# Two layers of attention and FFN on one core: in the second attention, two of four row tiles and of four probability tiles are transposed as 32x32 squares on VectorE and by DMA, and the last weights are loaded later, from GpSimd's queue

## The chip, the core and the metric

The kernel runs on one core of a Trainium2 chip. The metric is the device time of one execution in microseconds (us). The kernel before takes 454.63 us, the median of three runs (454.27 to 454.71).

## The reference

The input `x` is two sequences of 512 rows with 512 columns, float32. Two layers follow each other, and each is an attention and an FFN, each with a residual and a LayerNorm:

```
x = layernorm(x + L0_attn(x))     # memory read-out: elu(q)+1 against a given M and z, then Wo
x = layernorm(x + L0_ffn(x))      # ternary weights, silu(gate)*up, results truncated to int8
x = layernorm(x + L1_attn(x))     # one head of 128:
                                  #   q,k,v = x @ Wqkv + bqkv
                                  #   softmax(q k^T / sqrt(128)) v @ Wo + bo
x = layernorm(x + L1_ffn(x))      # (silu(x Wg^T) * (x Wu^T)) Wd^T, inner width 1376
```

The change is in the third line, `L1_attn`, and in when the weights of the fourth are loaded.

## The kernel before, in words

Everything is tiled by 128 partitions. A sequence `b` has four row tiles `xs[b][t]` (x_b_t below) of 128 rows by 512 columns; they stay in SBUF from the first layer to the last. The 1376 inner columns of the FFNs are 11 chunks, with weights `gu` (gate and up, 512 KB a chunk) and `wd` (down, 256 KB a chunk).

A matmul on TensorE contracts over the partitions, so a row tile has to be transposed before it can be multiplied with weights: its columns have to lie on the partitions. The kernel has two ways to do it.

- On TensorE: four 128x128 products with an identity into a PSUM bank, which VectorE or ScalarE copies to SBUF. `transposed` (L118) does so for four tiles of a sequence, 16 products.
- In squares: `nc.vector.transpose` turns each 32x32 square of a tile in its place, and `move_squares` (L301) moves the squares to where they belong, 16 DMAs of [32 partitions x tiles x 4 squares x 32 elements], one for each pair (i, j) of a source and a target group of 32 partitions. With `queues=3` the four DMAs with i == j are copies on VectorE instead, since these squares don't leave their partitions; four go on GpSimd's queue and eight on SyncE's. With `queues=2` the four go on GpSimd's queue too, which has eight then.

The stages around the change, in order:

1. The end of the first FFN (`f0_down`, `added`, `normed`, L888 to L990): for each row tile a down product on TensorE, truncation on ScalarE, sums and LayerNorm on VectorE, with the root on GpSimd. The first two tiles of sequence 0 are turned in squares (L963), the other two on TensorE (L981).
2. The second attention (L1128 to L1298), for b = 0 and then 1: queries and keys `pqk` (L1148), values `pv` (L1166), scores `psc` (L1099), their maxima on VectorE (`maxima`, L1102), exponentials on ScalarE (`exponentials`, L1111). Sequence 0's four probability tiles are turned in squares (L1180), sequence 1's rows and probabilities by `transposed` (L1131, L1287). `values` (L1206) multiplies the transposed probabilities with v into `pot`, `output` (L1228) the result with Wo, and `attended` (L1233) adds it to the row tile, divided by the sum of the exponentials. The bias `bo` is added to sequence 0's tiles by GpSimd (L1181) and to sequence 1's by four accumulating DMAs on GpSimd's queue (L1196), which stand behind a one-element copy `landed` (L1194) that reads what the last DMA of sequence 0's squares writes.
3. The second FFN (from L1299). Its products are done in three passes over operands that are split in an upper part (ScalarE) and rests (VectorE): `split_up` (L1056) for weights, `rows_room`, `turn_rows`, `rows_from_squares` for rows. The second sequence's rows are turned in squares again (`squares_r1`, L1308, `xt_f11`, L1315). `in_turn` is a chain that keeps VectorE's steps in a fixed order. A loop over `steps` (L1546) then goes through the chunks in the order of `turn` (L1046: 6 to 10, then 0 to 5), and splits weights two or more steps ahead of their use; the weights of chunk 2 are split after those of 6 to 10, 0 and 1, those of 3, 4 and 5 after that, and the down weights last.

The order of an engine's instructions is set when the program is built, by a scheduler; `with tc.issue_after(step)` puts what stands under it behind that step. GpSimd follows the program's own order. Each engine and each DMA queue runs its list in that order: an instruction that waits holds up what is behind it. DMAs of one queue use eight semaphores in turn.

The weights of the second FFN are loaded by SyncE: chunks 6 to 10 as soon as the first FFN has done with their room (L1009), then, behind the moves of sequence 0's first two tiles, all down weights and chunks 0 to 5 (L1011 to L1013). In SyncE's queue the moves of sequence 0's probabilities stand behind them.

Of the kernel before, what the change touches and what calls it, by code (L numbers as in the profile page):

```python
# [10 lines left out]
F32 = mybir.dt.float32  # L11
# [8 lines left out]
P = 128  # L20
B, S, HID = 2, 512, 512
NT = S // P
# [17 lines left out]
def kernel(  # L40
# [41 lines left out]
    def psum(name):  # L82
        return ps.tile([P, 512], F32, tag="mm", name=name)
# [152 lines left out]
    def branch(flag):  # L236
        return nc.values_load(flag[0:1, 0:1], engines=[PE], min_val=0, max_val=1)

    def up_weights(gu_in, name, chunks=range(len(CHUNKS))):
        gus = []  # L240
        for c in chunks:
            i, n = CHUNKS[c]
            gu = wffn.tile([P, 2, NK, n], F32, tag=f"gu{c}", name=f"gu{name}_{c}")
            at = 2 * HID * i
            nc.sync.dma_start(
                gu.rearrange("p a k i -> p (a k i)"),
                gu_in[at : at + 2 * HID * n].rearrange("(p f) -> p f", p=P),
            )
            gus.append(gu)
        return gus  # L250

    def down_weights(wd_in, name):
        wds = []
        for c, (i, n) in enumerate(CHUNKS):
            wd = wdp.tile([P, HID], F32, tag=f"wd{c}", name=f"wd{name}_{c}")
            nc.sync.dma_start(wd[:n], wd_in[i : i + n, :])
            if n < P:
                nc.gpsimd.memset(wd[n:], 0.0)
            wds.append(wd)
        return wds  # L260
# [497 lines left out]
    moved = move_squares(squares, xt1)  # L758
    wdp = ctx.enter_context(tc.tile_pool(name="wdp", bufs=1))
    with tc.issue_after(moved.ins):  # L760
        wds = down_weights(wd0_in, "0")
    with tc.tile_pool(name="f0", bufs=2) as f0:
        factors = {}

# [213 lines left out]
        for t in range(TURNED, NT):  # L978
            pt = psum(f"pt_a10_{t}")
            for k in range(NK):  # L980
                nc.tensor.transpose(pt[:, ts(k, P)], xs[0][t][:, ts(k, P)], ident)  # L981
            copies.append(
                nc.scalar.copy(xt_a10[1][:, t - TURNED], pt.rearrange("p (k i) -> p k i", k=NK))
            )
        added(i - 2)
        normed(i - 3)
        added(i - 1, behind=copies[-2:])
        normed(i - 2)
        for i in range(len(order), len(order) + 2):
            f0_down(i)  # L990

    def joined_weights(gu_in, c):

# [12 lines left out]
        nc.sync.dma_start(half.rearrange("p (k i) -> p k i", k=NK), up[:, :, : P // 2])  # L1006
        return full, half

    gus = up_weights(gu1_in, "1", range(6, len(CHUNKS) - 1))  # L1009
    gus.append(joined_weights(gu1_in, len(CHUNKS) - 1))  # L1010
    with tc.issue_after(moves_a.ins):  # L1011
        wds = down_weights(wd1_in, "1")
    gus = up_weights(gu1_in, "1", range(6)) + gus  # L1013

# [73 lines left out]

    probs = []

    def scores(b):

        qt, kt, _ = qkv[b]
        got = []
        for t in range(NT):
            p = psum(f"psc_{b}_{t}")
            nc.tensor.matmul(p, qt[:, ts(t, P)], kt, start=True, stop=True)  # L1099
            got.append((p, small.tile([P, 1], F32, tag="mx", name=f"mx_{b}_{t}", bufs=8)))  # L1100

        def maxima(tiles):  # L1102
            for t in tiles:
                p, mx = got[t]
                nc.vector.reduce_max(mx, p, AX.X)
                done = nc.vector.tensor_scalar_mul(mx, mx, -scale)
            return done

        return got, maxima

    def exponentials(b, got, behind={}):  # L1111
        sums = small.tile([P, NT], F32, tag="sums", name=f"sums_{b}")
        row = []
        for t, (p, mx) in enumerate(got):
            if t % 2 == 0:
                two = pair_tile(f"prob_{b}_{t}")
            e = two[:, t % 2, :]
            with ExitStack() as tied:
                if t in behind:
                    tied.enter_context(tc.issue_after(behind[t].ins))  # L1120
                moved = nc.scalar.activation(
                    e, p, AF.Exp, bias=mx, scale=scale, accum_out=sums[:, t : t + 1]
                )
            row.append(e)
        probs.append((row, sums))
        return moved

    qkv = []  # L1128
    for b in range(B):
        if b:  # L1130
            xt = transposed(xs[b], f"a1{b}")  # L1131
            with tc.issue_after(copies[-2].ins), tc.issue_after(copies[-1].ins):
                split_up(0, room0)
                split_up(1, room1[:6])
        qk = []
        qk2 = query_tile(f"qk_{b}")
        if b == 0:
            v2 = query_tile("v")
        pqk = [psum(f"pqk_{b}_{j}") for j in range(2)]
        for half in range(2 - b):  # L1140
            for j in range(2):
                for k in range(NK):
                    if b:
                        p, rows = pqk[j], xt[:, k, :]
                    else:
                        p = pqk[j].rearrange("p (h t i) -> p h t i", h=2, i=P)[:, half]
                        rows = xt_a10[half][:, :, k, :]
                    nc.tensor.matmul(  # L1148
                        p, wqkv[:, k, ts(j, D)], rows,
                        start=(k == 0), stop=(k == NK - 1),  # L1150
                    )
        for j, p in enumerate(pqk):
            s = qk2[:, j, :]
            moved = nc.scalar.activation(s, p, AF.Identity, bias=bqk[:, j : j + 1])
            qk.append(s)
        if b:
            pt0 = fp.tile([P, NT, NK, P], F32, tag="it10", name="pt_p0", bufs=1)
            move_squares(squares, pt0)
            pt0 = pt0.rearrange("p t k i -> p k t i")
        else:  # L1160
            table(AF.Exp, moved)
        v = v2[:, b, :].rearrange("p (t d) -> p t d", t=NT)
        for t in range(NT):
            p = psum(f"pv_{b}_{t}")
            for k in range(NK):
                nc.tensor.matmul(  # L1166
                    p[:, :D],
                    xt[:, k, ts(t, P)] if b else xt_a10[t // 2][:, t % 2, k, :],
                    wqkv[:, k, ts(2, D)],
                    start=(k == 0), stop=(k == NK - 1),  # L1170
                )
            nc.vector.tensor_add(v[:, t, :], bv, p[:, :D])
        qkv.append((qk[0], qk[1], v))
        if b == 0:
            got, maxima = scores(0)
            maxima(range(NT))
            exponentials(0, got)
            squares = fp.tile([P, NT, HID], F32, tag="it00", name="squares_p0", bufs=1)
            for t in range(NT):
                nc.vector.transpose(squares[:, t, :], probs[0][0][t])  # L1180
                nc.gpsimd.tensor_add(xs[0][t], xs[0][t], bo)  # L1181
# [5 lines left out]
            weight_upper(gus[turn[2]][:, a].rearrange("p k i -> p (k i)"), room2[3 * a])  # L1187

    got, maxima = scores(1)
    scaled_max = maxima(range(NT))  # L1190
    table(AF.Silu, exponentials(1, got))

    landed = small.tile([P, 1], F32, tag="off", name="landed")
    nc.gpsimd.tensor_copy(landed[2 * SQ : 3 * SQ], pt0[2 * SQ : 3 * SQ, NK - 1, NT - 1, P - 1 :])  # L1194
    for t in range(NT):
        nc.gpsimd.dma_start(xs[1][t], bo_in.to_broadcast([P, HID]), accum_op=ALU.add)  # L1196
    with tc.issue_after(scaled_max.ins):
        done = split_up(2, room2, True)
    with tc.issue_after(done.ins):
# [6 lines left out]
    def values(b, pt, cuts):  # L1206

        ot = ot2[:, b, :]
        w = S // cuts
        for i in range(cuts):  # L1210
            po = psum(f"pot_{b}_{i}")
            for k in range(NT):
                nc.tensor.matmul(  # L1213
# [70 lines left out]
        return pts, turned  # L1284

    values(0, pt0, 1)
    pt1 = transposed(probs[1][0], "p1").rearrange("p k (t i) -> p k t i", t=NT)  # L1287
    for t in range(NT):
        attended(0, t, output(0, t))
        norm_a1(0, t)  # L1290
    values(1, pt1, 2)
    for t in range(NT - 1):
        done = attended(1, t, output(1, t))
    rooms = [rows_room(0, "r0"), None]
    x3 = [row_blocks(rooms[0]), None]
    pts, turned = turn_rows(0)
    with tc.issue_after(turned.ins):
        p = output(1, NT - 1)  # L1298
    in_turn = Chain(done)  # L1299
    for pt, (h, m, _) in zip(pts, x3[0]):  # L1300
        in_turn(lambda: upper_lower(pt, h, m)[1])
    for t in range(NT - 1):
        in_turn(lambda: norm_a1(1, t))
    in_turn(lambda: attended(1, NT - 1, p))
    x = xs[1][NT - 1]
    stats = layernorm_stats(x, f"a11_{NT - 1}")
    in_turn.last = taken[f"a11_{NT - 1}"]
    squares = xtp.tile([P, NT, HID], F32, tag="xt", name="squares_r1")  # L1308
    for t in range(NT - 1):
        in_turn(lambda: nc.vector.transpose(squares[:, t, :], xs[1][t]))  # L1310
    in_turn(lambda: layernorm_apply(x, x, stats))
    in_turn(lambda: nc.vector.transpose(squares[:, NT - 1, :], x))
    for h, m, d in x3[0]:
        in_turn(lambda: crossed(d, h, m))
    xt_r1 = fp.tile([P, NT, NK, P], F32, tag="it10", name="xt_f11", bufs=1)  # L1315
# [230 lines left out]
    for i, (b, j) in enumerate(steps):  # L1546
# [6 lines left out]
            while len(held) > 1:  # L1553
                moved = finish_up()
        if i == 1:
            in_turn(lambda: split_up(AHEAD - 1, take(6)))
        elif i == 2:
            rooms[1] = rows_room(1, "r1")
            x3[1] = row_blocks(rooms[1])
            for k in range(NK):  # L1560
                with tc.issue_after(in_turn.last.ins):
                    uppers, in_turn.last = rows_from_squares(k)
        elif i == AHEAD:
            for h, m, d in x3[1]:
                in_turn(lambda: crossed(d, h, m))
# [80 lines left out]
```

## Time and profile before

| | |
|---|---|
| runs, median (lowest to highest) | 454.63 us (454.27 to 454.71) |
| the profiled execution's own time | 454.45 us |
| its span, first to last instruction | 452.7 us |
| TensorE clock granted (mean) | 0.999 |
| from 232.4 to 251.6 us: TensorE, VectorE, ScalarE, GpSimd busy | 19.20, 17.32, 10.11, 11.25 us |
| from 251.6 to 268.9 us: the same | 17.30, 14.83, 10.84, 3.95 us |
| DMA in the same two stretches | 136 and 40 GB/s |

A stretch's busy times tell which engine has room in it: TensorE has none in either, VectorE about two us in each, and GpSimd most of the second.

In the profile, PE is TensorE's matmuls and PEld its weight loads, DVE is VectorE, ACT ScalarE, POOL GpSimd, SP SyncE; a q behind the name is the engine's sequencer, which issues DMAs. L12 is line 12 of the kernel. Tile names are the program's, without the numbers behind an underscore: `pt_p` stands for the transposed probabilities of both sequences, PSUM and SBUF, `x<-in_bo` for the bias additions. A float32 product shows as two matmuls, so 16 transposes are x16 in the chain's rows, where each of them counts once, and 8 products of float32 by 512 columns are x16.

### The profile page before, as it was taken

The page shows a single profiled execution, that of the slowest core. Times are in us where ns is not written, and L with a number is a line of the kernel's source. Part 1 is how long each engine was busy: PE and PEld are TensorE (multiplying, and loading weights), DVE is VectorE, ACT ScalarE, POOL GpSimd, SP SyncE. Part 2 cuts the span into 40 slices and gives each one's busy share as a digit, 9 for nine tenths or more (in the row PEclk, how much of TensorE's full clock was granted, in tenths as well). Part 3 has the DMA queues.
Part 4 walks back from the last instruction along what each step waited for, and adds up shares of the span by engine and source line. Part 5 has one row for each costly group of instructions (what it writes and reads, how often), then busy time and mean ns, then how long its engine had stood idle before and what let it go on. Part 6 is the DMA issues. An engine that isn't in the chain of part 4 may idle for free.

```text
span 452.7 us, 5850 instructions
## 1 busy us (share of the span) xinstructions
PE 445.8 (98%) x1913; PEld 337.0 (74%) x1913; DVE 317.5 (70%) x634; ACT 259.7 (57%) x493; POOL 117.6 (26%) x164
## 2 busy tenths in 40 slices
PE   8999999999999999999999999999999999999995
PEld 8887753344587888888875578888888888888884
DVE  4976767877886898849898889545535447777524
ACT  5788995567467975567755645454645456442311
POOL 0300206566640059203384137000000000012111
PEclk9999999999999999999999999999999999999999
DMA  8999980020038001122784503200000000000101
GB/s 304 394 266 311 181 327 1 1 45 4 1 59 258 9 2 48 48 94 47 221 334 73 91 1 50 44 0 1 0 1 0 0 3 0 0 25 23 48 25 68
DMA packets 35604, 38.57 MB, mean 85 GB/s; under 512 B 23024, under 2 KB 23920, under 8 KB 35568
## 3 DMA queue, kind: packets, MB, share of 16 engines
q1 hardware_dynamic: 32912, 31.31, 21.0%
q0 software_dynamic: 2368, 6.42, 7.6%
q8 instruction: 22, 0.36, 0.3%
q10 hardware_dynamic: 288, 0.36, 0.2%
q14 instruction: 14, 0.11, 0.1%
HBM read 32.45 MB, written 2.10 MB: 76 GB/s over the span
## 4 chain that ended last, share of the span: by engine, by line
PE 97%; issue 1%; DVE 0%; ACT 0%; POOL 0%; POOLq 0%
PE pu L1338 24%; PE po L593 12%; PE pd L1338 12%; PE pq L538 9%; PE pg_f L789 9%; PE pu_f L789 9%; PE pd_f L848 4%; PE pqk L1148 3%; PE pu L1383 2%; PE pv L1166 2%; PE pot L1213 2%; PE psc L1099 2%; PE pmw L579 2%; PE po L1230 2%; PE pq L509 1%
## 5 line engine op out<-in xcount | busy, mean ns | idle before, releaser
L593 PE MATMUL po<-mw,q 128*128 128x512 f32 x128 | 56.9, 598 | 0.0
L1338 PE MATMUL pu<-r,ugu 128*128 128x512 f32 x200 | 48.6, 389 | 0.0
L146 POOL TENSOR_TENSOR rstd_f<-mv_f,ln_eps 128x1 f32<-128x1 f32 x15 | 6.0, 399 | 162.3 <-DVE mv_f L1506 128.7
L364 ACT ACTIVATE pu<-pu 128x512 f32<-128x512 f32 x42 | 24.1, 580 | 41.4 <-PE pu L1338 37.6
L593 PEld LDWEIGHTS po<-mw,q 128*128 128x128 f32 x128 | 22.8, 189 | 32.5 <-issue 15.9
L1338 PEld LDWEIGHTS pu<-r,ugu 128*128 128x128 f32 x200 | 37.5, 188 | 7.8
L615 DVE SCALAR_TENSOR_TENSOR x<-po,den,x 128x511 f32<-128x511 f32 x40 | 29.8, 745 | 1.9
L170 ACT ACTIVATE ta_f<-y_f,below_half 128x512 int8<-128x512 f32 (+1 forms) x22 | 15.9, 722 | 24.6 <-DVE y_f L158 22.2
L610 POOL TENSOR_TENSOR y<-y,y 128x511 f32<-128x511 f32 x16 | 21.3, 1332 | 23.5 <-ACT y L606 22.8
L1338 PE MATMUL pu<-r,it_early 128*128 128x512 f32 x104 | 24.9, 389 | 0.0
L1397 DVE TENSOR_TENSOR it_f<-ev,pu 128x512 f32<-128x512 f32 x20 | 13.7, 683 | 15.8 <-PE pu L1338 15.4
L1226 ACT ACTIVATE x<-x,off_f,rstd_f 128x512 f32<-128x512 f32 x7 | 5.7, 816 | 31.6 <-POOL off_f L1225 31.6
L815 DVE SCALAR_TENSOR_TENSOR it_f<-tb_f,ta_f 128x512 fp32r<-128x512 int16 (+1 forms) x22 | 15.6, 707 | 11.1 <-ACT tb_f L171 11.1
L1338 PEld LDWEIGHTS pu<-r,it_early 128*128 128x128 f32 x104 | 19.5, 188 | 4.0
L1338 PE MATMUL pd<-ugu,r 128*128 128x512 f32 (+1 forms) x79 | 22.5, 362 | 0.0
L789 PE MATMUL pg_f<-x,tu 128*128 128x512 f32 x88 | 22.1, 393 | 0.0
L789 PE MATMUL pu_f<-x,tu 128*128 128x512 f32 x88 | 21.7, 389 | 0.0
L376 POOL TENSOR_SCALAR td<-wd,inv_down 128x512 fp32r<-128x512 f32 x11 | 19.9, 1826 | 3.2 <-DVE inv_down L206 3.2
L848 PE MATMUL pd_f<-td,it_f 128*128 128x512 f32 x88 | 20.3, 389 | 0.0
L597 ACT ACTIVATE den<-po,den_eps 128x1 f32<-128x1 f32 x64 | 14.1, 271 | 10.5 <-PE po L593 10.5
L789 PEld LDWEIGHTS pg_f<-x,tu 128*128 128x128 f32 x88 | 16.4, 188 | 4.0 <-DVE x L615 0.4
L789 PEld LDWEIGHTS pu_f<-x,tu 128*128 128x128 f32 x88 | 16.5, 188 | 3.5
(396 smaller groups left out, 1117.0 us busy)
## 6 DMA issues: line engine op xcount, KB each, us to landing
gu<-in_gu SPq DMA_DIRECT2D x20, 512.0 KB, 7.0
wd<-in_wd SPq DMA_DIRECT2D x20, 256.0 KB, 4.8
wo<-in_wo SPq DMA_DIRECT2D x8, 512.0 KB, 9.1
wo<-in_wo POOLq DMA_DIRECT2D x8, 512.0 KB, 9.5
wq<-in_wq SPq DMA_DIRECT2D x8, 256.0 KB, 4.7
x<-in_x SPq DMA_DIRECT2D x7, 256.0 KB, 4.4
out<-x SPq DMA_DIRECT2D x7, 256.0 KB, 2.0
x<-in_bo POOLq DMA_DIRECT2D x4, 256.0 KB, 6.3
```

The source lines that it names most:

```text
L170: nc.scalar.activation(a[:n], y, AF.Relu, bias=below_half[:n])
L364: return nc.scalar.activation(p, p, AF.Copy, scale=BIG + 1.0)
L376: eng.tensor_scalar(out, w, factor, None, ALU.mult)
L538: done = nc.tensor.matmul(p, w, x, start=(start and i == 0), stop=(i == len(todo) - 1), skip_group_check=not start,)
L593: nc.tensor.matmul(po, qs[b][h0 + j][:, ts(t, P)], mw[:, h0 + j, :], start=True, stop=True,)
L597: nc.scalar.activation(den[:, j : j + 1], po[:, LAST:], AF.Identity, bias=den_eps)
L610: nc.gpsimd.tensor_add(ys[0][:, :LAST], ys[0][:, :LAST], y[:, :LAST])
L615: steps.append(nc.vector.scalar_tensor_tensor(x[:, :LAST], four[j][:, :LAST], d, x[:, :LAST], ALU.mult, ALU.add))
L789: nc.tensor.matmul(pp[a], t[:, a, i % NK, :], x2[b][i], start=(i == 0), stop=(i == 2 * NK - 1),)
L815: nc.vector.scalar_tensor_tensor(it[:n], tb[:n], 128.0, ta[:n], ALU.min, ALU.subtract)
L848: nc.tensor.matmul(pd, inter[b][c][:, ts(t, P)], td[c].bitcast(F32R), start=(c == 0), stop=(c == last),)
L1338: done = nc.tensor.matmul(p, w, x, start=(start and i == 0), stop=(i == n - 1), skip_group_check=not start,)
```

## The change

- Sequence 1's row tiles 0 and 1 are turned in squares: two transposes on VectorE behind their LayerNorms (L990, L995 of the kernel after), and `move_squares` with three queues. Tiles 2 and 3 are turned on TensorE, in a new function `turn_others`, which `scores(0)` calls between its first and second product. The products of queries and keys are done in halves of two tiles for both sequences, for sequence 1 the second half first.
- Sequence 1's probability tiles 0 and 1 are turned in squares too, between the maxima of the later tiles (L1206), and moved with two queues, behind the bias additions. Tiles 2 and 3 are turned on TensorE. `values(1)` does its second half first, and the row tiles of sequence 1 go on in the order 2, 3, 0, 1; the last one is now tile 1.
- Of the second FFN's weights, chunks 0 and 1 are loaded by SyncE behind the moves of sequence 1's rows. Chunks 2 to 5 and all down weights are loaded from GpSimd's queue, in the second step of the loop, behind a one-element copy `landed_r1` that reads an upper part of sequence 1's rows.

The table load for Silu stands behind a copy of the turned probabilities instead of the exponentials, and `split_up(AHEAD - 1)` is tied behind that copy.

```diff
-        normed(i - 3)
+        last_norm = normed(i - 3)
+        with tc.issue_after(last_norm.ins):
+            done = nc.vector.transpose(squares_a[:, 0, :], xs[1][0])
         added(i - 1, behind=copies[-2:])
-        normed(i - 2)
+        with tc.issue_after(done.ins):
+            last_norm = normed(i - 2)
+        with tc.issue_after(last_norm.ins):
+            nc.vector.transpose(squares_a[:, 1, :], xs[1][1])
         for i in range(len(order), len(order) + 2):
             f0_down(i)
+        moves_a = move_squares(squares_a[:, :TURNED], xt_a11[:, :TURNED])
...
     with tc.issue_after(moves_a.ins):
-        wds = down_weights(wd1_in, "1")
-    gus = up_weights(gu1_in, "1", range(6)) + gus
+        gus[:2] = up_weights(gu1_in, "1", range(2))
...
+    def turn_others(t):
+
+        if t != 1:
+            return
+        for t in range(TURNED, NT):
+            pt = psum(f"pt_a11_{t}")
+            for k in range(NK):
+                nc.tensor.transpose(pt[:, ts(k, P)], xs[1][t][:, ts(k, P)], ident)
+            copies.append(nc.scalar.copy(xt_a11[:, t], pt.rearrange("p (k i) -> p k i", k=NK)))
...
-            xt = transposed(xs[b], f"a1{b}")
...
-        for half in range(2 - b):
+        xt = [xt_a11[:, :TURNED], xt_a11[:, TURNED:]] if b else xt_a10
+        for half in (1, 0) if b else (0, 1):
...
     got, maxima = scores(1)
-    scaled_max = maxima(range(NT))
-    table(AF.Silu, exponentials(1, got))
+    squares1 = fp.tile([P, NT, HID], F32, tag="it00", name="squares_p1", bufs=1)
+    pt1 = xtp.tile([P, NT, NK, P], F32, tag="xt", name="xt_p1")
+    scaled_max = maxima(range(TURNED))
+    exponentials(1, got, range(TURNED))
+    for t in range(TURNED):
+        turned = nc.vector.transpose(squares1[:, t, :], probs[1][0][t])
+        with tc.issue_after(turned.ins):
+            scaled_max = maxima([TURNED + t])
+        exponentials(1, got, [TURNED + t])
...
     for t in range(NT):
         nc.gpsimd.dma_start(xs[1][t], bo_in.to_broadcast([P, HID]), accum_op=ALU.add)
+    move_squares(squares1[:, :TURNED], pt1[:, :TURNED], queues=2)
...
-    pt1 = transposed(probs[1][0], "p1").rearrange("p k (t i) -> p k t i", t=NT)
+    for t in range(TURNED, NT):
+        pt = psum(f"pt_p1_{t}")
+        for k in range(NK):
+            nc.tensor.transpose(pt[:, ts(k, P)], probs[1][0][t][:, ts(k, P)], ident)
+        move = nc.vector.tensor_copy if t % 2 else nc.scalar.copy
+        moved = move(pt1[:, t], pt.rearrange("p (k i) -> p k i", k=NK))
...
+            landed = small.tile([P, 1], F32, tag="off", name="landed_r1")
+            nc.gpsimd.tensor_copy(landed[:SQ], x3[1][NK - 1][0][:SQ, S - 1 :].bitcast(F32))
+            gus[2:6] = up_weights(gu1_in, "1", range(2, 6), nc.gpsimd)
+            wds = down_weights(wd1_in, "1", nc.gpsimd)
```

## The prediction, made before the result was known

> **What bounds the kernel now.** I read the page's busy shares and its chain of work that ended last first: is one engine the whole time?
>
> ```profile
> PE 445.8 (98%) x1913; PEld 337.0 (74%) x1913; DVE 317.5 (70%) x634; ACT 259.7 (57%) x493; POOL 117.6 (26%) x164
> ...
> PE 97%; issue 1%; DVE 0%; ACT 0%; POOL 0%; POOLq 0%
> ```
>
> TensorE works without a gap to 441.8 us, so each us it is spared ends the kernel a us earlier, as long as no operand comes late. Next the same chain in order of time, for the second attention (start, us, what):
>
> ```profile
> 232.38 3.44 PE psc L1099 x8
> 235.81 1.75 PE pt_a L128 x16
> 237.56 7.03 PE pqk L1148 x16
> 244.59 3.57 PE pv L1166 x32
> 248.16 3.44 PE psc L1099 x8
> 251.60 3.43 PE pot L1213 x8
> 255.03 1.75 PE pt_p L128 x16
> 256.78 3.44 PE po L1230 x8
> 260.21 3.45 PE pot L1213 x16
> ```
>
> The two 1.75 us rows, 16 transposes each (rows, then probabilities), are what the change halves. The last row is two halves; the second starts at 260.21 + 3.45/2 = 261.94. Third, GpSimd's timeline, because the new operand passes through its queue, and the answer for its line L1196:
>
> ```profile
> 239.70 2.61 POOL L316 DMA_DIRECT2D pt_p<-squares_p  x4 [2.48 <-DVE squares_p L1180]
> 246.33 0.18 POOL L1194 COPY landed<-pt_p 32x1 f32<-32x1 f32 x1 [4.02 <-DMA pt_p<-squares_p]
> 246.90 3.64 POOL L1196 DMA_DIRECT2D x<-in_bo  x4 [0.38 <-issue]
> ...
> 260.11 0.18 POOL L146 TENSOR_TENSOR rstd_a<-mv_a,ln_eps 128x1 f32<-128x1 f32 x1 [9.58 <-DVE mv_a L140]
> ```
>
> ```profile
> L1196 POOL DMA_DIRECT2D x<-in_bo x4: 958/1400/1908, 246.9 to 248.6; - x4
> ...
> DMA to landing us min/median/max: 4.3/6.3/7.9
> ```
>
> Four 256 KB bias additions by DMA start when the first sequence's squares have landed (246.3); the last starts at 248.6 and lands 7.9 us later, at 256.5. The DMA view of 250.5 to 255.0 shows them filling the 16 engines alone:
>
> ```profile
> q0 software_dynamic: 408, 0.75, 99.1%
> ```
>
> **The change, part by part.** Sums are made against the profiled execution: 454.45 us, a span of 452.7 and 1.75 around it, 0.18 under the runs' median of 454.63.
>
> *TensorE.* Sixteen of 32 transposes go: 2 x 1.75/2 = 1.75 us. The second QK goes from 8 products of 512 columns (7.03) to 16 of 256, which the first sequence's row prices at 6.91 (same line, x32): 0.12. Together 1.87 us, all on the path. If nothing is late, the moved half of the probabilities is wanted at 261.94 - 1.87 = 260.07.
>
> *Rows.* VectorE transposes of x_1_0 and x_1_1 go in at 227.2 and about 230.2. A 128x512 one holds it 0.63 (two in 1.29 at L1180). The last block copied in place (0.29, xt_a: four in 1.17) comes before the last statistics, the other three after the last norm. That norm, at 231.58 before, moves by 0.63 + 0.63 + 0.29 to 233.05. TensorE wants x_1_3 at 233.7: a stall of 0 to 0.3. The moves run 231 to 236 on SyncE (xt_a: eight in 5.74, landing 1.9 later) and 233 to 236 on GpSimd; they land by 238, wanted at 240.1. Hidden, with 2 us to spare.
>
> *First sequence's probabilities, unchanged but behind this.* Three more copies (0.87) put the first maximum at 235.4 instead of 233.27: +2.1. In ScalarE's new order three weight casts (L1026, four in 2.20) stand between exponentials 0 and 1 and a fourth before number 2. Exponential 1 goes from 235.05 to 238.6, number 3 ends at 241.5, the last transpose at 242.2 instead of 239.40: +2.8 (bounds 2.6 and 2.95). The two copies of transposed rows that VectorE did there (1.25) are gone and counted. Queued behind: the moves of these squares, then the "landed" copy, then the four bias additions, all on GpSimd. First squares landed 249.1 (TensorE wants them at 250.5: hidden); bias additions 249.7; last of them landed 256.5 + 2.8 = 259.3.
>
> *Second sequence's probabilities.* The two transposes end at about 252.6: first maximum at 249.0, since VectorE ends its delayed splits and v rows then, and maxima and transposes alternate. SyncE's eight moves run 252.7 to 257.8, landing by 259.7. GpSimd's eight are queued behind the bias additions. In the build each DMA of a queue waits for the earlier one on its semaphore, eight in turn; the fifth to eighth of these moves have the semaphores of the four bias additions. That such waits are real shows in SyncE's list of waits, where gu loads waited for wd loads five times, 2.8 us in total:
>
> ```profile
> SPq L245 <- DMA wd<-in_wd: 2.8, 5, 1.0
> ```
>
> So the eighth issues when the last addition has landed, 259.3, and lands 1.9 later (xt_a from GpSimd: median 2.1, later ones about 1.9). With 0.1 for the semaphore TensorE goes on at 261.35: a stall of 1.3 in place of the transposes.
>
> *Contention* has no row in this trace: SyncE's eight moves now run while the additions fill the engines. Lower bound 0. Upper: the DMA view of 212.7 to 219.8 (xt_a moves) gives q1 23.2% of 7.1 us, 1.65, and q0 8.7%, 0.6: 2.2 together, if all of it goes ahead of the additions. [...] I take 0.7: TensorE goes on at 262.05, against 261.94. Net +0.1.
>
> [...]
>
> *Engines off the path.* VectorE: 4 transposes (2.5) and 4 copies (1.2) in, 3 PSUM copies (1.95) out, 1.7 more; ScalarE one copy less. The copy of turned probabilities and x_0's sums move ahead with TensorE. The rstd steps of x_0 now stand behind the eighth move on GpSimd (260.0, before 260.11), four of 1.14 and a 0.8 norm: 265.5; TensorE wants them at 262.05 + 4.3 + 0.33 = 266.7. Hidden. Tile 1 as the last of the second sequence changes names, not counts.
>
> *Weights.* 15 loads (4 of 512 KB, 11 of 256: 4.9 MB) go from SyncE at 218.8 to 229 to GpSimd behind the second rows (their upper parts end at 290.8). On SyncE they were ahead of the first squares' moves, which waited for VectorE anyway; on GpSimd they pass x_0's bias, both squares, the additions, all rstd and the xt_f moves. At 0.9 per issue (additions) 14 us, at 1.9 28; data at the additions' 166 GB/s 30, at 380 13. So in by 304 to 321. First used: chunk 2 at 313.9, first in the queue and in by about 300 (a 512 KB load from GpSimd: 9.5); chunk 3 at 324.6, down weights from 345.8. Cost nothing; without that cover each late us counts in full. Two memsets (302.6 before) go behind them to about 316; their readers come after 370.
>
> **Rivals.**
> - *The moves are in time.* The additions land earlier than I think (the last transpose of the first probabilities late by 1.3, not 2.8, or they overlap better). TensorE's gaps are then 0 to 0.3: 454.63 - 1.87 = 452.8. For it: the additions' latency is a queue's, and may shrink. Against: +2.8 is a sum of rows.
> - *Contention in full, slower.* Place: the eighth move of the probabilities. Price 2.2 instead of 0.7, so TensorE goes on at 263.55: +1.6, 456.2. It is slower by over 0.2% from 1.5 us of contention on (262.85). For it: 99.1%; against: the 1.65 is spread over 252.7 to 258, partly after the additions' full stretch.
> - *Weights late*: chunk 2 after 314 would stall TensorE by the excess. Over 13 us of margin speak against it; 0.03, in the slower case.
>
> **Numbers.** About 0.2% (0.91 us) is what a measurement of this kernel can tell from no change. Likeliest, the stall eats the gain: 454.63 + 0.1 = 454.7, with 454.0 (no contention: -0.6) to 455.6 as its own range; 0.42. In time, or nearly: 0.30, from 452.8. Contention in full: 0.28, to 456.2. The range takes in the in-time case and nearly all of the slow one: 452.8 to 456.0.
>
> **What would show it.** In the profile after: rows of 0.87 at the two transposes; a gap of 1 to 3 us in TensorE ahead of the second half of pot, put down to a DMA of the turned probabilities; additions issued near 249.7; GpSimd's eighth move near 260 right after the last addition's landing; no wait on gu or wd after 300. If that gap isn't there, the total is near 452.8, and the chain from the last transpose of the first probabilities (242.2) is where I was wrong. If a gap stands at QK instead, the rows' moves were.

## The result, and the profile after

The changed kernel takes 457.42 us, the median of six runs (456.27 to 459.06), against 454.70 us for the kernel before on the same chip: a ratio of 1.0060, with a 95% interval of 1.0047 to 1.0073. It is slower by 2.7 us where 0.1 was predicted. The profiled execution of the changed kernel is the slowest of the six, 459.06 us, with a span of 457.28 against 452.67; the sums below are of this execution, and the median can't be taken apart in the same way.

From the page of the changed kernel, the busy line and the chain that ended last:

```profile
PE 446.6 (98%) x1913; PEld 339.8 (74%) x1913; DVE 318.2 (70%) x639; ACT 258.5 (57%) x492; POOL 132.6 (29%) x192
...
PE 94%; DMA 2%; issue 1%; DVE 0%; POOL 0%; ACT 0%; POOLq 0%
```

TensorE had 97% of the chain before and has 94% now, with 2% of DMA. That alone says little: a second profile of the kernel before, before_again, has 94% of TensorE and 1% of DMA too. TensorE's list of waits and the chain in order of time name the place (start, us, what):

```profile
PE pot L1232 <- DMA xt_p<-squares_p: 3.9, 1, 3.9
```

```profile
247.71 3.45 PE psc L1117 x8
251.16 0.04 issue
251.19 6.55 DMA x<-in_bo
257.74 0.28 issue
258.03 0.59 POOL xt_p L316
258.61 1.36 issue
259.98 0.01 POOLq L146
259.99 4.29 DMA xt_p<-squares_p
264.28 0.41 issue
264.69 3.33 PE pot L1232 x8
268.02 2.90 PE po L1249 x6
270.92 1.75 PE pt_f L1299 x16
```

It is the predicted place, the second half of pot, and the predicted cause, a bias addition and then a move of the probabilities. But the last move lands 4.29 us after its issue, not 1.9. And the work behind the gap takes longer than before: 3.33 instead of 1.73 for half a pot, 2.90 instead of 2.57 for the six products of po. The same rows of the kernel before:

```profile
261.94 1.73 PE pot L1213 x8
263.67 2.57 PE po L1230 x6
```

Stretches behind the gap show why (the number after POOL's is TensorE's granted clock):

```profile
264.60:266.00 1.40, 1.31 (x4) 1.14 (x5) 0.00 (x0) 1.07 (x2) 0.55 (x2) 0.69 0.00 0
266.00:268.00 2.00, 2.00 (x6) 1.55 (x6) 0.00 (x0) 0.09 (x1) 0.00 (x0) 0.50 0.00 0
268.00:269.00 1.00, 1.00 (x3) 0.35 (x2) 0.42 (x1) 0.00 (x0) 0.00 (x0) 0.73 0.00 0
269.00:271.00 2.00, 2.00 (x8) 0.95 (x7) 1.54 (x3) 0.00 (x0) 0.00 (x0) 1.00 0.02 4
```

Read in steps of 0.2 us, the clock is 0.50 from 265.1 to 268.5, 3.4 us. So the sum for this execution is: 1.87 saved, 3.93 of gap, 1.60 + 0.33 of longer products behind it, 0.17 that is left over (the last product ahead of the gap ends that much later than the sum has it), 0.52 that was lost by 221 us already, 0.07 less at the end: +4.61, which is the difference of the spans. Of the 1.93 of longer products, 0.24 is what half a pot takes more behind the gaps of filled_gap and after_again below, at full clock too (1.97); the other 1.69 is the clock's, and 3.4 us at half speed are 1.7.

**How the executions are compared.** By 221 us, at the first products of L981, ahead of the first of TensorE's products that the change touches, the sixteen profiles of this study stand 0 to 1.9 us behind the first one; the kernel before, profiled twice, stands at 0 and 0.84. It is lost in the first 11 us and between 62 and 97 us, in part in gaps at L593. I take it for jitter of an execution, and "place" below is TensorE's last product against that of the kernel before with it taken off. "Tail" is what follows that product; it was 5.62 us in both profiles of before. The ratios leave out one execution of the kernel before, of 926.7 us, and one of bias_split, of 1615.3.

| kernel | place | longest gap, from 221 us on | tail | median, ratio [95%] |
|---|---|---|---|---|
| changed | +4.16 | 3.93 pot | 5.55 | 1.0060 [1.0047, 1.0073] |
| after_again | +1.37 | 2.83 pot | 5.54 | one run |
| filled_gap | +1.95 | 1.17 pot | 5.56 | 1.0053 [1.0035, 1.0071] |
| no_lanes | +0.31 | 1.70 pot | 5.77 | 1.0048 [1.0028, 1.0068] |
| plain_loads | +9.66 | 8.17 pot | 5.54 | 1.0198 [1.0182, 1.0213] |
| bias_on_pool | +4.13 | 2.95 first pot | 5.77 | 1.0104 [1.0086, 1.0122] |
| bias_behind | +0.67 | 0.81 pt_f, twice | 5.55 | 1.0014 [0.9994, 1.0034] |
| bias_split | +0.64 | 0.67 first pot | 5.55 | 1.0034 [1.0022, 1.0045] |
| no_bias | -1.25 | 0.19 pt_f | 5.77 | 0.9990 [0.9976, 1.0004] |
| bias_spread | -1.19 | 0.19 pt_f | 5.55 | 0.9976 [0.9967, 0.9985] |
| rows_alone | -1.00 | none | 7.16 | 1.0016 [1.0007, 1.0024] |
| rows_padded | -0.98 | none | 7.81 | 1.0028 [1.0015, 1.0041] |
| probs_alone | +0.14 | 0.32 second QK | 5.77 | 1.0005 [0.9997, 1.0013] |
| weights_alone | +0.47 | 0.32 second QK | 6.83 | 1.0043 [1.0028, 1.0058] |

### The profile page after: what moved, and what is told of

The parts are those of the page before. It is cut to its first block, busy times and chain, and to the rows that moved or that the text cites. A ratio compares the mean times of both kernels' runs of the same rounds, so it can differ in the third digit from the quotient of the medians.

```text
span 457.3 us, 5917 instructions
## 1 busy us (share of the span) xinstructions
PE 446.6 (98%) x1913; PEld 339.8 (74%) x1913; DVE 318.2 (70%) x639; ACT 258.5 (57%) x492; POOL 132.6 (29%) x192
## 4 chain that ended last, share of the span: by engine, by line
PE 94%; DMA 2%; issue 1%; DVE 0%; POOL 0%; ACT 0%; POOLq 0%
PE pu L1368 23%; PE po L593 12%; PE pd L1368 12%; PE pq L538 9%; PE pg_f L789 9%; PE pu_f L789 9%; PE pd_f L848 4%; PE pqk L1159 3%; PE pu L1413 2%; PE pv L1177 2%; PE psc L1117 2%; PE pmw L579 2%; DMA x<-in_bo 1%; DMA xt_p<-squares_p 1%; PE pq L509 1%
## 5 line engine op out<-in xcount | busy, mean ns | idle before, releaser
L593 PE MATMUL po<-mw,q 128*128 128x512 f32 x128 | 56.9, 598 | 0.0
L593 PEld LDWEIGHTS po<-mw,q 128*128 128x128 f32 x128 | 22.8, 189 | 32.5 <-issue 15.9
L848 PEld LDWEIGHTS pd_f<-td,it_f 128*128 128x128 f32 x88 | 16.5, 188 | 3.4
```

The costliest lines, as they stand in the source:

```text
L593: nc.tensor.matmul(po, qs[b][h0 + j][:, ts(t, P)], mw[:, h0 + j, :], start=True, stop=True,)
L848: nc.tensor.matmul(pd, inter[b][c][:, ts(t, P)], td[c].bitcast(F32R), start=(c == 0), stop=(c == last),)
```

## The experiments

The theory behind the first of them: SyncE's moves do not slow the bias DMAs; the bias DMAs hold up the moves, all sixteen, and the long gap then costs a second time through the clock.

**Which part loses.** rows_alone turns only the rows in squares (the probabilities by `transposed`, as before), probs_alone only the probabilities; both load the weights late.

> Only the second sequence's rows are turned in squares; its probabilities are turned by TensorE as before; weights late as in the change. Theory (the rows' part does what it should; the loss is all in the probabilities' moves): TensorE saves 0.87 + 0.12 = 1.0 us, no gap at QK, no gap at pot: 453.5 to 454.0. Rival (the upstream 0.5 us and the delay of the first sequence's probabilities cost what the rows bring): 454.4 to 455.2. Second rival (late first probabilities stall TensorE at the first pot, at 250.5): a gap there, 455 or more.

> Only the second sequence's probabilities are turned in squares; its rows are turned by TensorE as before, so VectorE has no transposes and copies of them ahead of the first softmax; weights late as in the change. Theory (the moves starve until the bias DMAs have landed): the bias DMAs start near 246.9 as before and have landed by 256.5 to 257, before the moves are wanted at about 261; the moves land by 259 to 260.5, a gap of 0 to 0.5 us, 453.7 to 454.4. Rival (the moves are slow whatever lies beside them): a gap of 2 us or more at pot, 456 or more. Rival (contention charged in full on the additions): they land by 259, gap 0.5 to 1, 454.4 to 455.

rows_alone has no gap behind 221 us, and TensorE ends 1.00 us earlier, as summed; why the time is longer all the same (455.65 us, 1.0016 of the kernel before, where 453.5 to 454.0 was expected) is told below, at the tail. In probs_alone the bias DMAs start 2 us earlier than in the changed kernel (248.1), the last lands at 257.4, and the moves take a median of 2.3 us to land instead of 6.7; no gap at pot. Most of the 0.9 us that it should save is lost ahead of that: at the second QK TensorE waits for the copy of the turned rows, and 0.7 us goes there, which was not expected. So neither part alone makes the long wait; it needs the additions moved late by the rows' part and the moves of the probabilities' part.

**The bias DMAs left out.** In no_bias the four lines `nc.gpsimd.dma_start(xs[1][t], ...)` are gone, and nothing else is changed.

> The changed kernel without the four bias DMAs (the second sequence's output bias is left out, and nothing else). Theory: nothing else holds up the moves of the second probabilities. Each lands about 2 us after its issue, the last by 260.5 (plus the jitter of the first 75 us), no gap over 0.2 us in TensorE behind 220, granted clock 1.00 there; TensorE's last product 1.6 to 1.9 us ahead of where the kernel before has it, jitter set aside. The time depends on GpSimd's last drain too, which no rule so far foretells: 452.8 to 453.6 with a drain under 3.4 us, up to 455 with one of 5. Rival (sixteen moves of 128-byte pieces are slow side by side whatever else runs): a gap of 1 us or more stays at the second half of pot.

The answers for the turned tile, first of the changed kernel, then of no_bias (duration of the issue, then landing):

```profile
L316 SPq DMA_DIRECT2D xt_p<-squares_p x8: 585/630/991, 253.2 to 258.7; - x8
...
DMA to landing us min/median/max: 4.3/6.7/9.1
```

```profile
L316 SPq DMA_DIRECT2D xt_p<-squares_p x8: 586/609/613, 253.0 to 257.6; - x8
...
DMA to landing us min/median/max: 1.8/1.9/2.7
```

Issued at nearly the same times, they land in 1.9 us without the bias DMAs and in 6.7 with them, and TensorE has no gap at pot. In time the gain is small: a median of 454.45 where 452.8 to 453.6 was expected, since the place is 1.25 us ahead and not 1.6 to 1.9 (bias_spread, below, has the same loss) and the tail is 0.15 longer. The DMA view of four us shows how, from 253.5 in the changed kernel and then from 253.0 in no_bias (packets, MB, share of 16 engines; q1 is SyncE's queue, q0 GpSimd's):

```profile
q0 software_dynamic: 352, 0.64, 106.8%
q1 hardware_dynamic: 19, 0.00, 0.8%
```

```profile
q1 hardware_dynamic: 1097, 0.13, 20.4%
q0 software_dynamic: 144, 0.16, 18.8%
```

In those four us six moves are issued on SyncE, seven in no_bias, and 19 of their packets go, where 1097 go without the additions. They get going about when the third addition has landed (257.74), and the last of the sixteen lands 4.6 us behind the fourth addition (259.71). The additions themselves land as they did before, when no move was beside them (the kernel before: 4.3/6.3/7.9):

```profile
L1214 POOL DMA_DIRECT2D x<-in_bo x4: 963/1392/1896, 250.0 to 251.7; - x4
...
DMA to landing us min/median/max: 4.4/5.9/8.0
```

In the end the moves follow each other at about 0.2 us. In the trace each of these landings shows as sixteen completions, and of the last move's, fifteen are in by 263.23 and the sixteenth at 264.28. In the second profile of the changed kernel the same two stand at 263.74 and 263.86: one late completion makes most of the 1.10 us by which the gap is longer here.

**The semaphore that I had blamed.** no_lanes spreads the moves over three queues, so that GpSimd issues four (none waits for an addition's semaphore) and VectorE copies four:

```
-    move_squares(squares1[:, :TURNED], pt1[:, :TURNED], queues=2)
+    move_squares(squares1[:, :TURNED], pt1[:, :TURNED])
```

> The changed kernel with the sixteen moves of the second probabilities spread as those of its rows are: three queues' worth, four of them on GpSimd and four copied in place by VectorE, so that none of GpSimd's waits for the semaphore of a bias DMA. Theory (the engines are full of bias bytes, the moves starve until those have landed): the gap ahead of the second half of pot is still 2.5 to 3.9 us, 456.5 to 458.5. Rival of the prediction (the eighth move's wait for the last addition's semaphore sets the end): gap under 0.5 us, 453 to 454.

```profile
PE pot L1232 <- DMA xt_p<-squares_p: 1.7, 1, 1.7
```

The gap is 1.7, which neither expectation has; the median of 457.22 is in the theory's range. SyncE's first move, issued at 253.71, still lands at 260.95, behind the last addition (260.35), so the moves starve without that semaphore; twelve instead of sixteen of them then take 2.45 us. In the changed kernel the eighth move of GpSimd lands 0.2 behind the last of SyncE's: more than that the semaphore can't have cost by its own delay.

**Adding or bytes.** plain_loads makes the four DMAs plain loads into a tile that nobody reads (`dma_start(bo, ...)` without `accum_op`).

> The changed kernel with the four accumulating bias DMAs made plain loads of the same 256 KB from memory into a tile that nobody reads (the second sequence's output bias is left out). Queue, size and packets are kept, and only the adding is taken away. If it is the bytes of the software queue in the engines that hold the moves up: the moves again land about 9 us after the first is issued, a gap of 2 to 4 us, 456.3 to 458.5. If it is the adding (each packet reads, adds and writes in SBUF, and takes longer): loads land within 3 us of issue, moves by 260.5, gap under 0.5, 453 to 454. In between (loads at about half the additions' time): gap 0.5 to 2, 454 to 456.

The loads write one tile, so each waited for the one before (3.4 us each), and GpSimd's own moves stood behind them until 263.6: the total says nothing. Nor is only the adding taken away, as was expected: a load shows as 64 packets of 4 KB, an addition as 128 of 2 KB. But one thing can be read: SyncE's first move, issued at 254.21 as one load was just landing (254.33), landed in 1.9 us; the second, issued at 254.84 beside the next load, at 258.90, just behind that load (258.73). The eighth, beside the third load, did the same (262.62 behind 262.45). So a plain load of 256 KB held these moves up too, and the adding wasn't needed for it.

**The clock.** filled_gap puts ten products of 128x128 ones on TensorE ahead of the second half of pot.

> The changed kernel with ten more 128x128 products of a tile of ones on TensorE between the two halves of the second sequence's pot, about 2.2 us, whose result nobody reads: the wait for the moves stays, but TensorE isn't idle for it. Theory (the long gap costs twice: 3.9 us of waiting, then about 1.9 us since the granted clock falls to 0.50 for the next 3.5 us): the second half of pot starts when it did or a little later, then takes 1.73 and po 2.57 again; granted clock of 1.00 at 264 to 271; 456.0 to 456.8, faster than the changed kernel, and little spread from run to run. Rival (the clock's fall is by chance, or pot is slow because its operands are): the same 457.4 with the same spread, or slower by up to 2.2.

```profile
264.46 1.97 PE pot L1239 x8
266.43 2.58 PE po L1256 x6
269.00 1.75 PE pt_f L1306 x16
```

The moves landed as late as before (264.06), TensorE was idle for 1.17 at most, the clock stays at 1.00, and po has its old duration again (2.58); half a pot takes 1.97. So in these two executions the fall to 0.50 came with the idle gap (3.93 us) and not without it (1.17). In time, though, it is the rival that was right: the median is 457.5, no better than 457.42 (1.0053 and 1.0060 of the kernel before, beside which each ran), and the nine runs spread over 3.0 us where little spread was expected. The filled products don't help an execution whose clock would not have fallen. The second profile of the changed kernel was such a one:

> The changed kernel once more, for its profile alone. If the wait for the moves and the fall of the clock are the kernel's, a gap of 2.5 to 4.5 us at the second half of pot and, where it is over about 2.9, a granted clock of 0.50 for some 3.5 us behind it; where it is under that, no fall and a time of 456.3 to 456.9. If the fall is by chance, the two aren't tied. GpSimd's last drain: 2.2 us again if it is fixed by the kernel.

Its gap is 2.83, and the clock stays up, here in the row of the stretch behind it; in bias_on_pool a gap of 2.95 took it down (the last two fences):

```profile
PE pot L1232 <- DMA xt_p<-squares_p: 2.8, 1, 2.8
```

```profile
266.00:268.00 2.00, 2.00 (x7) 0.99 (x6) 1.19 (x3) 0.86 (x2) 0.27 (x1) 1.00 0.01 4
```

```profile
PE pot L1230 <- DVE v L1183: 3.0, 1, 3.0
```

```profile
257.00:258.00 1.00, 1.00 (x3) 0.48 (x2) 0.52 (x3) 1.00 (x3) 0.00 (x0) 0.50 0.00 0
```

Place +1.37 against +4.16: 1.10 from the gap, the rest, 1.69, from the clock. The spread of the six runs over 2.8 us goes with it in part: the mean granted clock was 0.995 or 0.996 in the three slowest and 1.000 and 0.998 in the two fastest. But it isn't the whole of it, since the two slowest runs of filled_gap, 459.20 and 459.47, have 0.999, and what made them slow is not shown.

**Three attempts to have the gain.** bias_on_pool adds the bias on GpSimd's datapath (`nc.gpsimd.tensor_add(xs[1][t], xs[1][t], bo)`) and leaves out the copy `landed`, bias_behind puts the four DMAs behind the moves, bias_split puts two of them right behind the rows' moves at 237.

> The four accumulating DMAs that add the output bias to the second sequence's rows (and the copy that waits for the first squares ahead of them) are replaced by four additions on GpSimd's own datapath; all else is the changed kernel. Theory (the moves of the second sequence's probabilities starve behind the bias DMAs): no traffic beside the moves, they land about 2 us after they are issued, by about 260, no gap ahead of the second half of pot (under 0.3 us), TensorE's clock stays at 1.00 there, and the time is 452.8 to 453.5, faster than before. Rival, semaphores alone (the eighth move waits for the last addition's semaphore): the same here, since the additions are gone from the queue. Rival, the squares are slow by themselves (128-byte pieces from 16 DMAs at once): a gap of 2 us or more stays, about 456. Bound from elsewhere: four GpSimd additions of 128x512 may hold up its moves, and VectorE beside them; then the gap is 0.5 to 2 us and the time 453.5 to 455.

> The changed kernel with one thing moved: the four bias DMAs stand behind the moves of the second sequence's probabilities on GpSimd's queue instead of ahead of them. Theory (the moves starve beside the bias DMAs, and only there): moves land some 2 us after they are issued, by 259 to 260.5, gap ahead of the second half of pot 0 to 0.5 us, granted clock 1.00; TensorE's last product ends 0.9 to 1.9 us before that of the kernel before; the time is 453.0 to 454.2 if the late additions (issued from about 258, landed by about 265 to 267) hold up nobody. Rival (squares slow by themselves): gap of 2 us or more, 456.5 or more. Rival (the gain is given back: second sequence's attended rows wait for the bias, then TensorE for them): no gap at pot, but one of 0.5 to 3 us at 266 to 275, 454.5 to 457.

> The changed kernel with two of the four bias DMAs moved forward: those of x_1_0 and x_1_1, whose rows VectorE has turned by 233, stand right behind the moves of the rows on GpSimd (about 236 to 238) instead of behind the copy that waits for the first probabilities; the other two stay. Theory (a full software queue starves the moves; late bias on GpSimd's queue holds up x_0's rstd): the first two land by about 242.5, before the first probabilities' moves; the other two land by about 256, the second probabilities' moves by 260.5; no gap over 0.3 us at either pot, none at pt_f, granted clock 1.00: TensorE's last product ends 1.2 to 1.9 us before that of the kernel before, up to 0.8 less from jitter in the first 75 us; 453.2 to 454.2, faster than before. Rival (the first two and the loads of gu run into the first probabilities' moves): a gap at the first pot, 250.5, of 0.5 to 2 us, 454.5 to 456. Rival (two additions starve the moves as four do): a gap of 1 us or more at the second half of pot, 455.5 or more.

None was faster. In the first two the moves land in a median of 1.9 us again, in bias_split in 3.8, still behind the last addition but with only 0.2 us of waiting at the second half of pot; all three run into another wait instead. bias_on_pool and bias_split hold up VectorE. The timelines of bias_split, GpSimd's and VectorE's:

```profile
237.06 1.91 POOL L1000 DMA_DIRECT2D x<-in_bo  x2
238.26 5.67 POOL L1194 TENSOR_TENSOR x<-x,bo 128x512 f32<-128x512 f32 x4
```

```profile
240.84 0.71 DVE L1193 STREAM_TRANSPOSE squares_p<-prob 128x512 f32<-128x512 f32 x1 [0.22 <-ACT prob L1139]
241.48 0.11 DVE L1126 TENSOR_SCALAR mx<-mx 128x1 f32<-128x1 f32 x1
241.51 2.98 DVE L1045 SCALAR_TENSOR_TENSOR it_early<-it_early,gu 128x512 fp32r<-128x512 f32 x1
```

The two early DMAs make x_0's four additions on GpSimd end 1.9 us later, so that the last of them meet VectorE's first weight split, which reads two tiles from SBUF and takes 2.98 instead of 0.68: it ends 0.6 us behind the last of them. The transpose beside them, with one input, takes its usual 0.7. In bias_on_pool the additions of x_1 do the same to a subtraction, the second of two in the first row: it takes 6.1 us and ends 0.6 behind the last of the four.

```profile
245.51 6.67 DVE L1044 TENSOR_TENSOR it_early<-it_early 128x512 fp32r<-128x512 f32 x2
246.69 4.92 POOL L1212 TENSOR_TENSOR x<-x,bo 128x512 f32<-128x512 f32 x4
```

TensorE's gap of 2.95 at the first pot and the fall of the clock behind it follow, and bias_on_pool is 1.0104. bias_behind has no gap at pot; there x_0's rstd steps stand behind the four issues:

```profile
258.45 3.68 POOL L1215 DMA_DIRECT2D x<-in_bo  x4
262.19 0.18 POOL L146 TENSOR_TENSOR rstd_a<-mv_a,ln_eps 128x1 f32<-128x1 f32 x1
```

They end at 266.8, and TensorE waits at pt_f. bias_spread puts x_1_0's DMA behind a norm's rstd at 232.5, x_1_2's and x_1_3's behind the moves, and x_1_1's behind x_0's rstd steps.

> The changed kernel with its four bias DMAs spread over GpSimd's idle places: x_1_0's behind the norm's rstd at about 230.5, x_1_2's and x_1_3's behind the moves of the second probabilities (about 258.5), x_1_1's behind x_0's four rstd steps (about 265). None stands ahead of a move that TensorE waits for, none ahead of x_0's additions on GpSimd. Theory: no gap over 0.3 us at the pots; x_0's rstd steps end by about 265, as VectorE's sums allow, so 0 to 0.7 us of waiting at pt_f; TensorE's last product 1.0 to 1.9 us ahead of the kernel before, jitter set aside; 453.0 to 454.0, faster than before. Rival (a late addition holds up VectorE's attended rows, and TensorE behind it): a gap of 0.5 to 2 us at 266 to 276, 454.3 to 456. Rival (the early one slows the moves of the rows): a gap at the second QK, about 240, of 0.5 to 1.5 us.

```profile
261.00:264.00 3.00, 3.00 (x15) 2.56 (x14) 3.00 (x8) 0.88 (x2) 2.53 (x8) 1.00 0.81 132
264.00:268.00 4.00, 3.81 (x17) 2.09 (x17) 2.91 (x6) 2.93 (x5) 2.66 (x7) 1.00 0.21 38
```

```profile
PE pt_f L1300 <- ACT x L1246: 0.2, 1, 0.2
```

The clock stays at 1.00 and nothing waits at pot: 453.96 us against 455.06, a ratio of 0.9976 [0.9967, 0.9985]. It does all the work and is faster than the kernel before, and by the ratios (1.0060) than the changed kernel. The place is -1.19 instead of -1.87, much as in no_bias: about 0.4 us is lost at pt_f, where the chain goes through x_0's rstd steps on GpSimd (0.2 of it as a wait), and the rest in pieces of 0.1 or less ahead of it.

**The weights and the tail.** weights_alone is the kernel before with only the fifteen loads moved to GpSimd.

> The kernel before with only the last weights' loads moved: fifteen loads go from SyncE to GpSimd, behind the second sequence's rows; nothing is turned in squares that wasn't. Theory (late weights cost nothing, TensorE never waits for gu or wd): the last product of TensorE at the same place within 0.5 us, the time within 0.3% of before. Rival (loads cost at their new place, by GpSimd's issue or by traffic beside the last rows): 0.5 to 1.5 us more, seen as a TensorE gap between 290 and 350. Second rival (taking 4.9 MB out of 218 to 250 frees the moves of the first probabilities and the bias DMAs): those land earlier by 0.5 to 2 us, which alone changes no time.

No gap in TensorE behind 280, so the late weights are in time; yet 2.0 us are lost. Two things show. A 0.52 us memset of wd stood ahead of x_0's additions on GpSimd and went with the loads, so the first addition now meets x_1_3's norm on VectorE. The norm in before, beside the memset, then in weights_alone, beside the addition; in the changed kernel, with neither beside it, it takes 0.55:

```profile
231.58 0.83 DVE L152 TENSOR_SCALAR x<-x,mv_f,rstd_f 128x512 f32<-128x512 f32 x1 [0.71 <-POOL rstd_f L147]
```

```profile
232.79 1.48 DVE L152 TENSOR_SCALAR x<-x,mv_f,rstd_f 128x512 f32<-128x512 f32 x1 [0.71 <-POOL rstd_f L147]
```

TensorE's list of waits shows 0.3 at QK for it, there and in probs_alone, and the place is 0.47 later. Another 1.2 is the tail, which makes 1.7 in this profile: GpSimd ends each execution with a drain, which the page does not count as work. It took 3.59 us in before, 4.81 here, 5.14 in rows_alone, 3.75 in probs_alone, 2.20 in the changed kernel. Begun 3.4 us ahead of the last output's landing (448.26 and 451.68 in before, 452.94 and 456.35 in the changed kernel), it sets the end where it is longer. That is where rows_alone's gain of 1.00 went (tail 7.16 instead of 5.62). I took it for a matter of how many DMAs GpSimd had issued and added eight of 512 bytes to rows_alone, 59 in all as in the changed kernel; before_again asked if it is fixed.

> The kernel with only the rows in squares, plus eight 512-byte DMAs on GpSimd behind the weights' loads (into a scrap tile that nobody reads), so that GpSimd issues 59 DMAs in all, as the changed kernel does, instead of 51. In the profiles so far GpSimd's last drain took 2.20 us with 59 DMAs, 3.75 with 55, 5.14 with 51, 4.81 with 47 and 3.59 with 32, and it ends the span where it takes more than about 3.4. If it goes by the number of DMAs: drain of 2.2 us, last outputs landed set the end again, 1.4 to 1.6 us less than with the rows alone: 453.6 to 454.4. If it goes by bytes or by what the DMAs are: 5.1 again and no gain, 455.4 to 455.9.

> The kernel before once more, for its profile alone. If what the changed kernels have lost by 75 us (0 to 1.5 us in nine profiles, waits for ScalarE and VectorE at lines that the change doesn't touch) is jitter of each execution, this profile has some of it too, 0.2 to 1.2 us; if it is the changed kernels' own, the second scores begin at 248.1 to 248.2 here as in the first profile. GpSimd's last drain: 3.6 us again if it is fixed by the kernel.

It came out the same in both profiles of a kernel (3.59 again in before, 2.20 again in the changed one), but it doesn't go by the number: rows_padded, with 59 too, drained for 5.79 us, and its tail is 0.65 longer than that of rows_alone. What it goes by stays open.

## Why the prediction was wrong, point by point

- **TensorE saves 1.87: right, or nearly.** rows_alone shows the first 1.00 of it exactly; in no_bias 1.75 is saved when po begins.
- **Rows hidden: right.** No gap at QK; x_1_3's norm delayed nothing. (The sum for its start gives 233.13, not 233.05; measured 233.34, with 0.5 of jitter.)
- **First probabilities and additions: right.** Predicted issue of the first addition 249.7, of landing of the last 259.3; measured 249.98 and 259.71, with the same 0.5.
- **Contention: the step that failed.** I charged 0.7 between bounds of 0 and 2.2, an estimate that no run shows, and let the eighth move land 1.9 behind the last addition. That prices what the moves take from the additions, and not what the additions take from the moves. The additions lost nothing (4.4/5.9/8.0 us to landing, where before had 4.3/6.3/7.9); SyncE's moves did, with 19 packets where 1097 go otherwise. The 1.9 was a row for one move on free engines, and here all sixteen were left to do: 4.6 us behind the last addition (3.05 in the second profile, 2.45 for twelve moves). So TensorE went on at 264.17, jitter set aside, where I had 262.05: 2.1 us. In the second profile it was 1.0. In the four us from 253.5 the trace has 352 packets of GpSimd's queue at 0.19 us each, and the 19 of SyncE's at 0.03. Why SyncE's moves hardly went stays open.
- **The wait of the eighth move for a semaphore: there, but worth 0.2 us at most**, not the cause. The 0.1 that I added for the semaphore has no row; the profile after has 0.28 from the fourth addition's landing (259.71) to the eighth issue (259.99), and 0.41 from the last landing (264.28) to the product.
- **Not in the sum at all: the clock.** I priced every gap at its length. Here 2.83 us of gap cost nothing more (after_again), and 3.93 brought a clock of 0.50 for 3.4 us, which is 1.7 us of work. With the 2.1 above, and 0.24 for half a pot behind a gap, that is the way from the predicted +0.1 to a place of +4.16. By my own numbers contention in full was a gap of 3.5 us (263.55 less 260.07), between the 2.95 and the 3.93 that took the clock down in these runs, and the sum had no term for it.
- **rstd of x_0 hidden, with 1.2 to spare: right for the changed kernel, where the gap covers it.** But it costs 0.4 in the runs without that gap, and "the moves are in time", 452.8, left that out.
- **Weights: right for the changed kernel** (no wait behind 280), but they are not without effect: what they take along on GpSimd's queue, and the drain, made 1.7 of the 2.0 us in weights_alone.
- **The rivals.** "Contention in full" comes nearest: TensorE on at 263.55, where 264.69 less 0.52 of jitter was measured, 264.17. With the clock's 1.7 it would have given 457.9 instead of 456.2, beside runs from 456.3 to 459.1. It stood as contention on the additions, though, and that is not what happened: its nearness is luck.

## What to carry to other kernels

Where several large DMAs of GpSimd's queue were in flight (four additions of 256 KB), the small moves of these runs on another queue hardly went: 19 packets in four us, 1097 without the additions. Count such moves as starting when the large ones have landed, and put their whole number behind that (sixteen took 4.6 us behind the last addition), not one latency (1.9). A TensorE gap like the longest of these runs is to be priced twice, once for its length and once for the clock that may fall behind it: 2.95, 3.93 and 8.17 us brought 0.50 for 3.4 us or more, 2.83 did not. Before an operation is moved on GpSimd's queue, look at what moves with it: which VectorE instruction its neighbours meet then (beside GpSimd's additions two with two SBUF inputs took 2.98 and 6.1 us instead of 0.68, and the norm's tensor_scalar 1.48 instead of 0.55), and how long the last drain becomes (2.20 to 5.79 us here).

## What the runs showed of the hardware that I had not expected

- Gaps of 1.17, 1.70 and 2.83 us left TensorE's clock at 1.00; 2.95, 3.93 and 8.17 took it to 0.50. No threshold follows from one execution each: the fall came 3.3, 4.4 and 4.0 us after the idle time had begun, in the first two some 0.4 us after the products had gone on. It lasted 3.4, 3.4 and 10.2 us.
- Beside GpSimd's additions two of VectorE's operations with two SBUF inputs took 2.98 us (bias_split) and 6.1 (bias_on_pool) instead of 0.68, and each ended 0.6 behind the last addition; the 6.1 spans four additions in a row. One with a single tensor as input, the norm, was held up too (weights_alone), 0.55 to 1.48; a transpose beside the additions of bias_split was not, 0.71.
- GpSimd's last drain took 2.20 (the changed kernel) to 5.79 us (rows_padded), the same each time in the two kernels profiled twice, and set the end of the execution where it was over 3.4.
